# A graph layer on one core: the order of its head is rewritten

## The chip, the cores and the metric

The kernel runs on one NeuronCore of a Trainium2 chip. A core has TensorE (PE, matrix products; its weight loads are shown as PEld), VectorE (DVE), ScalarE (ACT), GpSimd (POOL) and SyncE (SP), which here only issues DMAs. All engines run their own instructions in order and wait for each other on semaphores; 16 DMA engines move data between device memory and the core's memory (SBUF). The metric is the device time of one execution in microseconds (us).

## The reference

A layer of a graph network over 3125 nodes with 256 channels and 103125 edges, in float32. The edges come sorted by their destination `dst`. What is computed, with names shortened:

```python
xn  = layernorm(x)                                   # per node
agg = segment_sum(xn[src], dst, 3125)                # sum over a node's incoming edges
h   = relu(agg @ W_rel + b_rel + xn @ W_root)        # 256 -> 512
i, f, g, o = split(h @ W_ih.T + b_ih + b_hh, 4)      # 512 -> 4 x 512, f is not used
hl  = sigmoid(o) * tanh(sigmoid(i) * tanh(g))
x   = x + (hl @ W_fc + b_fc) + mix(xn)               # mix: 8 heads, k and v normed, q @ (k^T v) / N + xn
# then a mixture of 8 experts, top 2 of a softmax per node, on layernorm(x):
x   = x + sum over the node's two experts of weight * (gelu(xe @ W1 + b1) @ W2 + b2)
```

## The kernel before, in words

The nodes are cut into 25 tiles of 126 (`T`, `P`). The aggregation is a matrix product: for a chunk of 252 destinations (13 chunks, the last shorter), a matrix `A` holds, for each pair of a source and a destination, how many edges join them, and the aggregated channels are the sum over the 25 source tiles of `xn^T A`. To keep float32's precision, `xn` is split into `hi` and `lo`, two operands of a reduced type, so each tile takes four products of 126x252 (L630: two halves of the channels, `hi` and `lo`).

`A` is built on the chip from lists of edges. Destinations are taken in groups of six, 525 groups in all, and each group may have up to 256 edges. `build` (L379 to L394) makes three groups' part of `A`: two comparisons on VectorE (L384, `hr` of sources and `hk` of keys), six products on PE (L390), one copy on ScalarE (L392). A chunk needs 14 builds. `hr` and `hk` have two buffers each, so VectorE can be at most two builds ahead of PE.

What stands ahead of the first chunk is called the head here. It does four things at once:

- **Loads.** SP loads `raw` (dst and src as a table of 128 rows with 808 edges each), the nodes `xn` in five loads of five tiles, `W_root`, `firsts` (row 0 of that table, the first edge of every column, copied to 105 partitions), `behind` and a dozen small vectors. They stand on SP's queue in the order of the program (L156 to L230).
- **Norms.** `norm(b)` (L343) normalizes five tiles: five pairs of L194 and L195 for the moments, a square root on ScalarE (L197), a reciprocal (L198), five writes (L349), and a store of the tiles to device memory. `rounded(b)` (L353) makes `hi` on ScalarE; L436 makes `lo` on VectorE.
- **Root products.** `root(t0)` (L358) takes four tiles: eight transposes on PE (L366), two copies on ScalarE (L368), then for each of four quarters `m` of the 512 channels a product in four passes on PE (L373) and a copy with the bias on ScalarE (L376), and stores of `xT` and of the four quarters to device memory (L369, L377). There are seven, the last with one tile. Products land in one of three PSUM buffers (`ps_mm`), shared with the builds; transposes in one of two (`ps_tr`), shared with those of the lists; the quarters wait in six buffers `hr` for their stores.
- **Lists.** `find()` (L236) is a generator that makes the lists of edges in steps, each ended by a `yield`. Step one: `raw` as float32 (L248), transposed on PE (L254) and stored as `ends_dram` in the order of the edges (L263, L265). Step two: five scans over `firsts` (L275) count on VectorE, for each group, the columns that begin below it; `at_i` is the column in which it starts, and five gathers on POOL (L283) fetch those columns as `near`. Step three: five scans over `near` (L289) give the exact first edge `begin_i` (L292), and five more gathers (L297) fetch each group's 256 edges as `both`. Step four, the rest: for each of the five sets of 105 groups, six operations on VectorE turn `both` into the tile of the source, the source within its tile and a key (L307 to L316); `order` and `wrong` (L321 to L324) check that the edges are sorted and no group is over-full; PE sums `wrong` over the partitions (L326), and `total_f`, `off` are made of it (L328, L330); then per set four transposes on PE (L336), and copies to `rowT` on ScalarE (L338) and `keyT` on VectorE (L340), which reads `off`.

The order of the work on an engine is made by a scheduler that takes the program's order as priority and issues what is ready by its own estimate. `tc.issue_after(ins)` puts all instructions of its block that run on the engine of `ins` behind it. In the head of the kernel before (L404 to L441) it is used three times: the first norm behind the store of `ends_dram`, step two behind the first norm's last write, the second norm behind `at_i`. `pins` hands such instructions out of `find`.

Behind the head, for every chunk, PE runs the 100 products of L630 with the 14 builds of the next chunk between them. VectorE and ScalarE also run the mixing part there, from a queue of steps keyed by chunk and build: `fetch` loads five tiles `q` from `xn_dram` (L510, from SP), `means` (L517) sums them on VectorE behind the twelfth build of the first chunk. At the end of each second chunk SP writes a blank part of `xs_dram` (7 MB). Weights for the network part behind the chunks, `wrel`, `wih` (three loads) and `wfc`, 4 MB together, are loaded from SP after the head's program (L445 to L452), into memory that the head's tiles have left.

Of the kernel before, what the change touches and what calls it, by code (L numbers as in the profile page):

```python
# [9 lines left out]
F32 = mybir.dt.float32  # L10
# [4 lines left out]
OP = mybir.AluOpType  # L15
AX = mybir.AxisListType

N = 3125
C = 256
P = 126  # L20
T = 25
# [42 lines left out]
def gps_layer(  # L64
# [90 lines left out]

    nc.sync.dma_start(raw[:, 0, :], dst)  # L156
    nc.sync.dma_start(raw[:, 1, :], src)
    for b in range(T // TB):
        load_nodes(xn[:, b * TB:(b + 1) * TB, :], b * TB, (b + 1) * TB)
        if b == 0:  # L160
            nc.sync.dma_start(wroot, W_root.rearrange("(k p) m -> p k m", p=128))
            nc.sync.dma_start(firsts, dst[0:1, :].to_broadcast([GP, NCP]))
            brel = columns_of(b_rel, KH, "brel")
# [73 lines left out]
    def find():  # L237
# [8 lines left out]
        for i in range(2):  # L246
            ends = sp.tile([128, NCP], F32, name="ends", tag="ends", bufs=2)
            nc.scalar.copy(ends, raw[:, i, :])  # L248
            for r in range(0, nr, 4):
                pt = ps_tr()  # L250
                m = min(4, nr - r)
                for j in range(m):
                    w = min(128, NCP - 128 * (r + j))
                    nc.tensor.transpose(pt[:w, 128 * j:128 * j + 128],  # L254
                                        ends[:, 128 * (r + j):128 * (r + j) + w], ident)
                whole_ = m if NCP >= 128 * (r + m) else m - 1
                if whole_:
                    nc.scalar.copy(rows[:, r:r + whole_, :, i],
                                   pt[:, :whole_ * 128].rearrange("p (r e) -> p r e", e=128))
                if whole_ < m:  # L260
                    nc.scalar.copy(rows[:left, r + whole_, :, i],
                                   pt[:left, whole_ * 128:m * 128])
# [10 lines left out]
        scr = sp.tile([GP, NCP], F32, name="scr", tag="ends", bufs=2)  # L273
# [18 lines left out]
        nc.vector.scalar_tensor_tensor(begin_i, at, 128.0, below, op0=OP.mult, op1=OP.add)  # L292
# [27 lines left out]
        order = sp.tile([128, NCP], F32, name="order", tag="ends", bufs=2)  # L320
# [3 lines left out]
        nc.vector.tensor_reduce(wrong[:, 1:2], full, AX.X, OP.add)  # L324
# [33 lines left out]
    def root(t0):  # L358
# [11 lines left out]
        for m in range(KH):  # L370
            pm = ps_mm()
            for k in range(KC):
                nc.tensor.matmul(pm[:, :n], wroot[:, k, 128 * m:128 * m + 128], xt[:, k, :n],  # L373
                                 start=(k == 0), stop=(k == KC - 1))
            hr = np_.tile([128, TQ * P], F32, name="hr", bufs=6)
            nc.scalar.activation(hr[:, :n], pm[:, :n], AF.Identity, bias=brel[:, m:m + 1])  # L376
            nc.sync.dma_start(root_dram[:, m, t0 * P:t0 * P + n], hr[:, :n])  # L377
# [25 lines left out]

    pins = []  # L404
    steps = find()
    next(steps)
    with tc.issue_after(pins.pop().ins):
        normed = norm(0)
    with tc.issue_after(normed.ins):
        next(steps)  # L410
    root(0)
    rounded(0)
    with tc.issue_after(pins.pop().ins):
        norm(1)
    next(steps)
# [3 lines left out]
    norm(2)  # L419
    root(2 * TQ)  # L420
    rounded(2)
    for _ in steps:
        pass
    norm(3)
    rounded(3)
    norm(4)
# [4 lines left out]
    root(3 * TQ)  # L431
    for _ in range(2):
        next(parts)
# [3 lines left out]
    for t0 in range(4 * TQ, T, TQ):  # L437
        root(t0)
        for _ in range(5):
            next(parts, None)  # L440
# [4 lines left out]
    nc.sync.dma_start(wrel, W_rel.rearrange("(k p) m -> p k m", p=128))  # L445
    wih = gl.tile([128, KH, 3, DH], F32, name="wih")

    wv = W_ihT.rearrange("(k p) m -> p k m", p=128)
    for i, gate in enumerate((0, 2, 3)):
        nc.sync.dma_start(wih[:, :, i, :], wv[:, :, gate * DH:(gate + 1) * DH])  # L450
    wfc = gl.tile([128, KH, C], F32, name="wfc")
    nc.sync.dma_start(wfc, W_fc.rearrange("(k p) m -> p k m", p=128))  # L452
# [663 lines left out]
```

## Time and profile before

| | us |
|---|---|
| median of 5 runs | 1148.34 (1147.43 to 1148.81) |
| the profiled execution's own time | 1152.27 |
| span of the profile, first to last instruction | 1150.5 |
| PE busy over the span | 1058.8 (92%) |
| DVE / ACT / POOL busy | 553.6 / 427.7 / 170.5 |
| mean granted TensorE clock | 0.966 |
| first product of the aggregation (L630) | 96.14 |
| start of chunks 2, 3 and 4 | 115.18, 133.78, 155.31 |

How to read the lines that follow: each names the start and the length in us, the engine (SPq and the like are an engine's DMA issues), the line of the kernel, the operation, `out<-in` with shapes, a count, and in brackets how long the engine had idled before and what ended that. In rows by stage, each engine's busy time is followed by its count of instructions in brackets; "PEclk" or the granted clock is the share of its full speed that TensorE was given. A copy is "lands" when its semaphore shows the last of its parts.

### The profile page before, as it was taken

The page shows a single profiled execution, that of the slowest core. Times are in us where ns is not written, and L with a number is a line of the kernel's source. Part 1 is how long each engine was busy: PE and PEld are TensorE (multiplying, and loading weights), DVE is VectorE, ACT ScalarE, POOL GpSimd, SP SyncE. Part 2 cuts the span into 40 slices and gives each one's busy share as a digit, 9 for nine tenths or more (in the row PEclk, how much of TensorE's full clock was granted, in tenths as well). Part 3 has the DMA queues.
Part 4 walks back from the last instruction along what each step waited for, and adds up shares of the span by engine and source line. Part 5 has one row for each costly group of instructions (what it writes and reads, how often), then busy time and mean ns, then how long its engine had stood idle before and what let it go on. Part 6 is the DMA issues. An engine that isn't in the chain of part 4 may idle for free. (4 is left out here: it accounts for less than half of the span.)

```text
span 1150.5 us, 15551 instructions
## 1 busy us (share of the span) xinstructions
PE 1058.8 (92%) x5613; PEld 809.1 (70%) x5613; DVE 553.6 (48%) x1767; ACT 427.7 (37%) x936; POOL 170.5 (15%) x153
## 2 busy tenths in 40 slices
PE   5799999999999999999999997399999999999992
PEld 3358998998995454555555457288888888788781
DVE  5757788787751183939393927411112222221210
ACT  3454754764722233333333336122222222223120
POOL 2220000000001002020202022112222212221221
PEclk9799999999999999999999999599999999999996
DMA  7983964872008321212121111157666667766734
GB/s 230 302 290 107 252 199 115 234 209 57 1 1 282 131 91 37 90 38 91 37 91 38 35 38 58 40 169 202 192 191 189 183 205 207 215 188 161 225 66 124
DMA packets 121148, 161.43 MB, mean 140 GB/s; under 512 B 9570, under 2 KB 109320, under 8 KB 120870
## 3 DMA queue, kind: packets, MB, share of 16 engines
q1 hardware_dynamic: 108156, 144.40, 39.9%
q0 software_dynamic: 12064, 15.08, 7.0%
q8 instruction: 49, 0.80, 0.3%
q10 hardware_dynamic: 840, 0.83, 0.2%
q14 instruction: 39, 0.32, 0.1%
HBM read 101.37 MB, written 62.10 MB: 142 GB/s over the span
## 5 line engine op out<-in xcount | busy, mean ns | idle before, releaser
L747 PE MATMUL ps_mm<-hT,wih 128*128 128x504 f32 (+1 forms) x672 | 259.3, 546 | 0.1
L747 PEld LDWEIGHTS ps_mm<-hT,wih 128*128 128x128 f32 x672 | 121.8, 193 | 132.3 <-issue 127.9
L1020 PE MATMUL ps_mm<-xe,w 128*128 128x256 f32 (+1 forms) x896 | 190.5, 371 | 3.5 <-DVE xe L1014 3.5
L1033 PE MATMUL ps_o<-w,hf 128*128 128x256 f32 x832 | 184.2, 379 | 0.0
L1020 PEld LDWEIGHTS ps_mm<-xe,w 128*128 128x128 f32 x896 | 162.5, 193 | 27.5 <-DVE xe L1014 6.8
L630 PE MATMUL ps_o<-A,hi 126*128 126x252 f32 (+1 forms) x650 | 175.8, 304 | 0.8 <-ACT A L392 0.7
L1033 PEld LDWEIGHTS ps_o<-w,hf 128*128 128x128 f32 x832 | 157.8, 190 | 21.3
L630 PE MATMUL ps_o<-A,lo 126*128 126x252 f32 (+1 forms) x650 | 160.9, 280 | 0.0
L1022 ACT ACTIVATE hf<-ps_mm,sm 128x256 f32<-128x256 f32 (+1 forms) x160 | 71.7, 453 | 201.7 <-PE ps_mm L1020 200.0
L392 ACT CAST A<-ps_mm 126x450 fp32r<-126x450 f32 x175 | 93.8, 538 | 99.7 <-PE ps_mm L390 98.1
L1038 POOL DMA_INDIRECT acc_dram<-y,xs x52 | 80.4, 1546 | 322.4 <-DVE y L1037 114.4
L630 PEld LDWEIGHTS ps_o<-A,hi 126*128 126x128 f32 x650 | 124.4, 191 | 2.8 <-ACT aggT L638 1.7
L384 DVE TENSOR_TENSOR hr<-two,rowT 128x756 bf16<-128x756 bf16 x175 | 95.8, 548 | 62.0 <-PE ps_mm L390 61.5
L630 PEld LDWEIGHTS ps_o<-A,lo 126*128 126x128 f32 x650 | 124.9, 192 | 0.0
L390 PE MATMUL ps_mm<-hk,hr 128*126 128x150 bf16 x1050 | 102.5, 233 | 12.7 <-DVE hk L384 12.4
L384 DVE TENSOR_TENSOR hk<-two,keyT 128x900 bf16<-128x900 bf16 x175 | 108.7, 621 | 0.0
L390 PEld LDWEIGHTS <-hr 128*126 128x126 bf16 x1050 | 91.9, 138 | 18.5 <-DVE hk L384 16.5
L1036 DVE TENSOR_TENSOR y<-ps_o,b2s 128x256 f32<-128x256 f32 x52 | 22.1, 425 | 158.7 <-PE ps_o L1033 158.7
L749 ACT ACTIVATE act<-ps_mm,bg 128x504 f32<-128x504 f32 (+1 forms) x84 | 52.6, 634 | 107.3 <-PE ps_mm L747 96.4
L795 DVE SCALAR_TENSOR_TENSOR scr<-xl,wrows 126x256 f32<-126x256 f32 x160 | 75.5, 472 | 3.3
L872 POOL DMA_INDIRECT xs_dram<-rows,at_i x50 | 52.7, 1053 | 128.3 <-DVE at_i L869 110.5
L1022 ACT ACTIVATE hf<-ps_mm,small 128x256 f32<-128x256 f32 x64 | 29.9, 474 | 77.1 <-PE ps_mm L1020 77.1
(250 smaller groups left out, 919.4 us busy)
## 6 DMA issues: line engine op xcount, KB each, us to landing
w<-in_W_dram SPq DMA_DIRECT2D x56, 1024.0 KB
xs_dram<-blank SPq DMA_DIRECT2D x3, 7022.5 KB
xs_dram<-blank SPq DMA_DIRECT2D x1, 6757.5 KB
xs<-xs_dram SPq DMA_DIRECT2D x24, 265.0 KB
root_dram<-hr SPq DMA_DIRECT2D x24, 252.0 KB
root<-root_dram SPq DMA_DIRECT2D x6, 1008.0 KB
b2s<-in_b_dram SPq DMA_DIRECT2D x28, 128.0 KB
xn_dram<-xn SPq DMA_DIRECT2D x5, 630.0 KB
```

The costliest lines, as they stand in the source:

```text
L384: row = nc.vector.tensor_tensor(to[:, :m], two[:, :, :w, :].to_broadcast([128, m, w, GH]), of[:, g:g + m, None, :].to_broadcast([128, m, w ...
L390: mm = nc.tensor.matmul(pa[:P, i * DT:(i + 1) * DT], hr[:, i, :, h], hk[:, i, :, h], start=(h == 0), stop=(h == GH - 1))
L392: copy = nc.scalar.copy(A[:, :, c0:c0 + m * D], pa[:P, :m * DT].rearrange("p (d t) -> p t d", t=T))
L630: last = nc.tensor.matmul(pg[k][:, :n], of[:, t, 128 * k:128 * k + 128], A[:, t, :n], start=(t == 0 and of is hi), stop=(t == T - 1 and of ...
L747: mm = nc.tensor.matmul(pm[:, :n], wih[:, k, i, 128 * m:128 * m + 128], hT[:, k, :n], start=(k == 0), stop=(k == KH - 1))
L749: nc.scalar.activation(act[:, i, :n], pm[:, :n], AF.Tanh if gate == 2 else AF.Sigmoid, bias=bg[:, gate, m:m + 1])
L795: nc.vector.scalar_tensor_tensor(scr, xl[:, i, :], 1.0, wrows[:, e, :], op0=OP.mult, op1=OP.mult, accum_out=lg[:, i, e:e + 1])
L872: put = nc.gpsimd.indirect_dma_start(out=xs_dram[:, :], out_offset=bass.IndirectOffsetOnAxis(ap=at_i[:w, i:i + 1], axis=0), in_=rows[:w, i ...
L1020: nc.tensor.matmul(pm, w1[:, k, 128 * m:128 * m + 128], xe[:, k, :], start=(k == 0), stop=(k == KC - 1))
L1022: nc.scalar.activation(hf[:, m, :], pm, AF.Gelu, bias=b1s[:, m:m + 1])
L1033: nc.tensor.matmul(po, hf[:, m, 128 * h:128 * h + 128], w2[:, m, :], start=(m == 0), stop=(m == KF - 1))
L1038: nc.gpsimd.indirect_dma_start(out=acc_dram[:, :], out_offset=bass.IndirectOffsetOnAxis(ap=xs[:, h, C + NE:].bitcast(I32), axis=0), in_=y, ...
```

## The change

Six edits, all in the head.

1. `firsts` is loaded first on SP, ahead of `raw`; before, it stood behind the first load of nodes and `W_root`.
2. `ends`, `scr` and `order` share three buffers instead of two, so that the scans of `firsts` need not wait for the transposes of `ends`.
3. The chain of orders is longer (`then(ins, do, ...)` runs a step behind an instruction). The scans and the gathers of `near` come straight behind the store of `ends_dram` in the program, without a wait for a norm; norm 0 is put behind `at_i`, norm 1 behind the last write of norm 0, the step of `begin_i` and the gathers of `both` behind the last write of norm 1, norm 2 behind `begin_i`, norm 3 behind norm 2, the work on `both` behind norm 3, norm 4 behind the last operation on `wrong`.
4. `find` has one more `yield`, behind `wrong`; what follows it (the sum on PE, the transposes of the lists, `rowT`, `keyT`) is put, on PE, behind the second quarter of the fourth root product (`root(3 * TQ, lambda: ...)`), so it stands in the middle of that product.
5. The builds of the first chunk: before, 2 behind the fourth root product and 5 behind each later one; now 3 inside and 3 behind the fifth, 5 inside and 3 behind the sixth, none around the last.
6. The loads of `wrel`, `wih` and `wfc` are put on SP behind the last store of the last root product.

In the order that results, VectorE runs the five scans of `firsts` ahead of the first norm; a `lo` (L444) stands inside norm 1, one between the last scan of `near` and `begin_i`, one inside norm 3, one ahead of `total_f`; on SP the store of `xn` from norm 3 stands ahead of the third root product's stores, and the five weight loads stand ahead of the first two loads of `q`; on POOL the gathers of `both` stand ahead of the additions for `bg` and the copies to `small`. Behind the head every engine's order is the same as before. Lines move by up to 10: L373 is L375, L349 is L351, L436 is L444, L384 is L390, L517 is L526, L630 is L639.

```diff
@@ -153,13 +153,13 @@
         nc.sync.dma_start(of, ap)
         return of
 
+    nc.sync.dma_start(firsts, dst[0:1, :].to_broadcast([GP, NCP]))
     nc.sync.dma_start(raw[:, 0, :], dst)
     nc.sync.dma_start(raw[:, 1, :], src)
     for b in range(T // TB):
         load_nodes(xn[:, b * TB:(b + 1) * TB, :], b * TB, (b + 1) * TB)
         if b == 0:
             nc.sync.dma_start(wroot, W_root.rearrange("(k p) m -> p k m", p=128))
-            nc.sync.dma_start(firsts, dst[0:1, :].to_broadcast([GP, NCP]))
             brel = columns_of(b_rel, KH, "brel")
 
     nc.sync.dma_start(behind[:112, :], dst[1:113, :])
@@ -244,7 +244,7 @@
         nc.gpsimd.memset(rows[:, nf, :, 0], float(FAR))
         nc.gpsimd.memset(rows[:, nf, :, 1], 0.0)
         for i in range(2):
-            ends = sp.tile([128, NCP], F32, name="ends", tag="ends", bufs=2)
+            ends = sp.tile([128, NCP], F32, name="ends", tag="ends", bufs=3)
             nc.scalar.copy(ends, raw[:, i, :])
             for r in range(0, nr, 4):
                 pt = ps_tr()
@@ -270,7 +270,7 @@
 
 
         below = sp.tile([GP, GQ], F32, name="below")
-        scr = sp.tile([GP, NCP], F32, name="scr", tag="ends", bufs=2)
+        scr = sp.tile([GP, NCP], F32, name="scr", tag="ends", bufs=3)
         for q in range(GQ):
             nc.vector.tensor_scalar(scr, firsts, limit[:, q:q + 1], None, op0=OP.is_lt, op1=OP.add,
                                     accum_out=below[:, q:q + 1])
@@ -289,7 +289,8 @@
             nc.vector.tensor_scalar(scr[:, :128], near[:, q, :, 0], limit[:, q:q + 1], None,
                                     op0=OP.is_lt, op1=OP.add, accum_out=below[:, q:q + 1])
         begin_i = sp.tile([GP, GQ], I32, name="begin_i")
-        nc.vector.scalar_tensor_tensor(begin_i, at, 128.0, below, op0=OP.mult, op1=OP.add)
+        pins.append(nc.vector.scalar_tensor_tensor(begin_i, at, 128.0, below,
+                                                   op0=OP.mult, op1=OP.add))
 
 
         both = sp.tile([GP, GQ, GE, 2], F32, name="both", tag="both")
@@ -317,11 +318,12 @@
                                            op0=OP.mult, op1=OP.add)
 
         wrong = const.tile([128, 2], F32, name="wrong")
-        order = sp.tile([128, NCP], F32, name="order", tag="ends", bufs=2)
+        order = sp.tile([128, NCP], F32, name="order", tag="ends", bufs=3)
         nc.vector.tensor_tensor(order, raw[:, 0, :], behind, OP.is_gt)
         nc.vector.tensor_reduce(wrong[:, 0:1], order, AX.X, OP.add)
 
-        nc.vector.tensor_reduce(wrong[:, 1:2], full, AX.X, OP.add)
+        pins.append(nc.vector.tensor_reduce(wrong[:, 1:2], full, AX.X, OP.add))
+        yield
         pw = ps_tr()
         nc.tensor.matmul(pw[:, :2], ones, wrong, start=True, stop=True)
         total_f = const.tile([128, 1], F32, name="total_f")
@@ -355,7 +357,7 @@
         s = slice(TB * b, TB * b + TB)
         nc.scalar.copy(hi[:, s, :], xn[:, s, :])
 
-    def root(t0):
+    def root(t0, between=None):
 
         ts = range(t0, min(T, t0 + TQ))
         n = len(ts) * P
@@ -370,11 +372,15 @@
         for m in range(KH):
             pm = ps_mm()
             for k in range(KC):
-                nc.tensor.matmul(pm[:, :n], wroot[:, k, 128 * m:128 * m + 128], xt[:, k, :n],
-                                 start=(k == 0), stop=(k == KC - 1))
+                mm = nc.tensor.matmul(pm[:, :n], wroot[:, k, 128 * m:128 * m + 128], xt[:, k, :n],
+                                      start=(k == 0), stop=(k == KC - 1))
             hr = np_.tile([128, TQ * P], F32, name="hr", bufs=6)
             nc.scalar.activation(hr[:, :n], pm[:, :n], AF.Identity, bias=brel[:, m:m + 1])
-            nc.sync.dma_start(root_dram[:, m, t0 * P:t0 * P + n], hr[:, :n])
+            store = nc.sync.dma_start(root_dram[:, m, t0 * P:t0 * P + n], hr[:, :n])
+            if between and m == KH // 2 - 1:
+                with tc.issue_after(mm.ins):
+                    between()
+        return store
 
     def build(A, g, c0, m):
 
@@ -401,55 +407,58 @@
         for d in range(d0, d1, BANK * D):
             yield build(A, d // D, d - d0, min(BANK, (d1 - d) // D))
 
+    def then(ins, do, *of):
+
+        with tc.issue_after(ins.ins):
+            return do(*of)
+
+
     pins = []
     steps = find()
     next(steps)
+    stored = pins.pop()
+    next(steps)
     with tc.issue_after(pins.pop().ins):
-        normed = norm(0)
-    with tc.issue_after(normed.ins):
-        next(steps)
+        last = then(stored, norm, 0)
     root(0)
     rounded(0)
-    with tc.issue_after(pins.pop().ins):
-        norm(1)
-    next(steps)
+    last = then(last, norm, 1)
+    then(last, next, steps)
     nc.vector.tensor_copy(two[:, 0], two_f[:, :, None].to_broadcast([128, DT, GH]))
     root(TQ)
     rounded(1)
-    norm(2)
+    last = then(pins.pop(), norm, 2)
+    last = then(last, norm, 3)
     root(2 * TQ)
     rounded(2)
-    for _ in steps:
-        pass
-    norm(3)
     rounded(3)
-    norm(4)
+    then(last, next, steps)
+    root(3 * TQ, lambda: next(steps, None))
+    then(pins.pop(), norm, 4)
     rounded(4)
     found.close()
 
     parts = builds(A0, 0)
-    root(3 * TQ)
-    for _ in range(2):
-        next(parts)
     for b in range(T // TB):
         u = slice(b * TB, b * TB + TB)
         nc.vector.tensor_tensor(lo[:, u, :], xn[:, u, :], hi[:, u, :], OP.subtract)
-    for t0 in range(4 * TQ, T, TQ):
-        root(t0)
-        for _ in range(5):
+    for t0, n in zip(range(4 * TQ, T, TQ), (3, 5, 0)):
+        stored = root(t0, lambda: [next(parts) for _ in range(n)])
+        for _ in range(3):
             next(parts, None)
     nodes.close()
 
     gl = ctx.enter_context(tc.tile_pool(name="gl", bufs=1, side="right"))
     wrel = gl.tile([128, KC, DH], F32, name="wrel")
-    nc.sync.dma_start(wrel, W_rel.rearrange("(k p) m -> p k m", p=128))
     wih = gl.tile([128, KH, 3, DH], F32, name="wih")
+    wfc = gl.tile([128, KH, C], F32, name="wfc")
 
     wv = W_ihT.rearrange("(k p) m -> p k m", p=128)
-    for i, gate in enumerate((0, 2, 3)):
-        nc.sync.dma_start(wih[:, :, i, :], wv[:, :, gate * DH:(gate + 1) * DH])
-    wfc = gl.tile([128, KH, C], F32, name="wfc")
-    nc.sync.dma_start(wfc, W_fc.rearrange("(k p) m -> p k m", p=128))
+    with tc.issue_after(stored.ins):
+        nc.sync.dma_start(wrel, W_rel.rearrange("(k p) m -> p k m", p=128))
+        for i, gate in enumerate((0, 2, 3)):
+            nc.sync.dma_start(wih[:, :, i, :], wv[:, :, gate * DH:(gate + 1) * DH])
+        nc.sync.dma_start(wfc, W_fc.rearrange("(k p) m -> p k m", p=128))
 
 
     wrT = gl.tile([NE, C], F32, name="wrT")
```

## The prediction

> **What bounds the kernel now.** I read the page's slices first, then the order of time over the first 115 us, then busy time by stage, and last the landings in the trace's semaphore events.
>
> ```profile
> PE   5799999999999999999999997399999999999992
> PEclk9799999999999999999999999599999999999996
> ```
>
> A slice is 28.8 us. TensorE is nearly full behind the third slice; the first three are the head. By stage, PE is busy 9.02 + 16.74 + 14.37 + 19.50 + 13.73 = 73.4 of the first 96 us, so at most 22.6 us are there to gain. The order of time shows what PE waits for:
>
> ```profile
> 10.06 0.75 DVE L194 BATCH_NORM_STATS2 bn<-xn 126x6 f32<-126x256 f32 x2 [7.81 <-DMA xn<-in_x_dram]
> ...
> 14.58 1.05 DVE L275 TENSOR_SCALAR_CACHE_REDUCE scr<-firsts,limit 105x808 f32<-105x808 int32 x1
> ...
> 22.05 1.20 POOL L283 DMA_INDIRECT near<-ends_dram,at_i  x1 [19.83 <-DVE bn L194]
> ...
> 33.57 0.18 DVE L292 SCALAR_TENSOR_TENSOR begin_i<-at,below 105x5 int32<-105x5 f32 x1
> ...
> 50.28 0.15 DVE L324 TENSOR_REDUCE wrong<-full 128x1 f32<-128x5 f32 x1
> ...
> 58.89 0.43 DVE L340 TENSOR_SCALAR keyT<-ps_tr,off 128x210 bf16<-128x210 f32 x1
> ...
> 60.27 8.02 PE L373 MATMUL ps_mm<-xt,wroot 128*128 128x504 f32 x16
> ...
> 96.14 0.39 PE L630 MATMUL ps_o<-A,hi 126*128 126x252 f32 x1 [0.65 <-ACT A L392]
> ```
>
> VectorE idles until 10.06, then does the scans of `firsts`, then the list chain (first gather 22.05, `begin_i` 33.57, `wrong` 50.28, last `keyT` 58.89), with norms between. The third product ends at 48.65 and the fourth starts only at 60.27, behind the lists. The first aggregation is at 96.14. Busy time by stage adds the clock (columns: PE, PEld, DVE, ACT, POOL busy, granted clock, DMA share, GB/s):
>
> ```profile
> 24.93:28.34 3.41, 1.82 (x7) 0.61 (x5) 1.61 (x9) 0.09 (x1) 2.80 (x3) 1.00 0.40 107
> 28.34:31.75 3.41, 1.74 (x6) 1.34 (x7) 2.51 (x13) 2.79 (x4) 0.14 (x1) 0.50 0.66 161
> 48.82:52.23 3.41, 0.90 (x6) 0.76 (x6) 3.41 (x15) 0.62 (x2) 0.00 (x0) 1.00 0.99 339
> 52.23:55.65 3.42, 0.99 (x5) 0.67 (x5) 3.42 (x13) 2.28 (x4) 0.00 (x0) 0.50 0.79 287
> ```
>
> A stretch of 3.41 us with PE about half busy is followed by one at half clock, where a pass of L373 takes 0.84 us for 0.42.
>
> What comes after the head is needed too, since the change moves loads there:
>
> ```profile
> 97.02 0.89 SPq L510 DMA_DIRECT2D q<-xn_dram  x2
> ...
> 110.00 1.48 DVE L517 TENSOR_REDUCE hmean<-q 126x40 f32<-126x1280 f32 x1
> ...
> 112.74 0.63 PE L390 MATMUL ps_mm<-hk,hr 128*126 128x150 bf16 x6 [0.59 <-DVE hk L384]
> ```
>
> `hmean` runs 13.9 us behind the first aggregation, and PE already waits 0.59 us for the build behind it: VectorE has no slack there.
>
> **The change part by part.** The new program's order on each engine is known; I put the durations above into it. Root products are counted 0 to 6.
>
> *`firsts` first.* `raw` of dst landed at 4.08, that of src, equally large, at 5.38: 404 KB in 1.30 us. The 331 KB ahead of them cost 1.07 us: dst 5.15, src 6.45, the first `xn` 11.1 for 10.06. `firsts` itself lands near 3.9, and its five scans (1.09 apart), `two` 0.2 and `at`, `at_i` 0.4 end at 10.0 instead of 21.7, in time when VectorE was idle. Root 0 starts at 17.5 (16.49), ends at 26.3 (25.83).
>
> *Norms in one piece.* Norm 1 could follow norm 0 at 15.6, but its load landed at 19.26; it starts there (21.63 before). Stats 2.0, one `lo` 1.4 that the new order puts inside, square root and reciprocal 0.65, five writes 1.6: done at 24.9 (28.9). PE goes from root 0 to root 1: transposes to 27.4, ScalarE's copies behind one `hi` and three `hr` to 28.5, product 28.5 to 35.3 (31.32 to 39.66).
>
> *The gathers.* `ends_dram` landed at 18.77, now about 19.8; `near` starts there instead of 22.05. The slowest DMA channel of SP's queue was behind until 26.53, and the first gather landed on it at 26.70. I take 26.7 to 27.5 for all five. Bounds: 2.6 us behind each issue (other channels in this trace), or the last at 32.2 as before. Scans end at 28.7, a `lo` of 1.4 stands ahead of `begin_i`: 30.3 (33.57). `both` follows on POOL at 30.6 (34.57), now ahead of `bg` and `small`, for which nothing on the path waits.
>
> *Norms 2 and 3.* Both now stand behind `begin_i`. Norm 2 from 30.3, first write 2.9 later as in norm 0 (10.06 to 12.96), last at 34.9. ScalarE's `hi` follows to 36.1, then a `lo` inside norm 3 to 37.9; norm 3's square root is at 38.1, and on ScalarE the last `hr` of root 1 and the copies for root 2 are queued behind it. So root 2 starts at 39.4 (41.53), after 3 us of idle PE. By the rows above that costs the clock: at half rate to about 45.4, end 49.2 (48.65). Kept, it would end at 46.2.
>
> *Lists behind norm 3, transposes inside root 3.* Norm 3 ends at 40.3. `both` landed 4.9, 7.2, 10.6, 12.8 and 13.8 us behind its first issue; from 30.6 the last is in at 44.4, and five groups of 1.4 to 1.6 us, `order` 1.8 and `wrong` end at 49.5 (50.28) without waiting for it. Root 3 starts at 51.2; its first eight passes end at 54.6, and only there the sum of `wrong` is taken on PE. `total_f` comes at 55.0 (53.11), the last `keyT` 5.8 us later as before: 60.8 (58.89). The other eight passes, 3.4 us, run between the list transposes. Root 3 ends at 60.8, not 67.7. This is where the gain lies: the lists end later than before, but a root product is behind PE by then.
>
> *The rest of the head.* From root 4's first transposes (68.97) to 96.14 were 27.2 us. Added are two builds that stood ahead (0.84) and 0.6 where groups of 3, 3, 5, 3 builds wait for VectorE oftener than 2, 5, 5, 2; the wait of 0.65 at the end goes, as root 6 now stands behind the last build. 60.9 + 27.2 + 0.84 + 0.6 − 0.65 = 88.9. Gain of the head: 96.14 − 88.9 = 7.2 us.
>
> *The weights behind the last store.* `wrel`, `wih` and `wfc`, 4096 KB, leave the head, where SP's stores no longer queue behind them; by these times no `hr` buffer waits longer. But on SP they now stand ahead of `q`. Before, the last store of `root_dram` was issued at 95.17 and `q` landed at 101.42: 6.25 us, of which 1.85 the wait for the store. Loads moved 300 (`wih` behind `wrel`) to 350 KB/us: 12 to 14 us more. The last store is now 0.6 us behind the first aggregation, so `q` is in at 0.6 + 6.25 − 1.85 + 12 to 14 = 17.0 to 19.0, and `hmean` was due at 13.9. Builds for the second chunk stand behind it on VectorE, PE behind those: 3.1 to 5.1 us lost, 4.1 taken. Bounds: nothing, if `q` is not held up; 9.7, in the second rival.
>
> The skill's page "DMA: Bandwidth & Descriptors", section "Queues, rings and completion order", says that a DMA engine takes a queue's descriptors in ring order, which speaks against this edit. The trace has it for loads only (the two `q` at 101.42 and 103.39, in order); by the rule 4.1 us are lost, with no such order up to nothing, and the sum would be 1141.1.
>
> **Sum.** 7.2 − 4.1 = 3.1 us faster. Profiled: span 1150.5, time 1152.27, 3.9 above the median of the runs; the difference goes to the median: 1148.34 − 3.1 = 1145.2.
>
> The skill's page "TensorE: Matmul & The Clock Gate", Part 1, says that the clock drops after an idle window of about 3.4 us. The trace drops it after a half busy one (1.82 of 3.41, above). By the rule root 2 would stay at full clock and end at 46.2, root 3's half would be at 51.7, `total_f` be set by VectorE at 53.0, and the sum be 2.0 us lower, 1143.2.
>
> **The rivals.**
> *The gathers land early* (2.6 us behind each issue) and the clock holds in root 2. For it: channels other than the slowest did so. Against: the slowest decides. `begin_i` 29.3, root 2 a microsecond earlier, and 2.0 for the clock: 3.0 more, 1142.2.
> *The weights hold the builds longer* (other side). If they move at the 263 GB/s of the stage from 70 to 80 us, they take 16.0 us and `q` lands at 21; `hmean` is 7.1 late, and PE, idle that long, pays one and a half windows of half clock, 2.6. 9.7 − 7.2 = 2.5 slower: 1150.8. It decides from a loss of 7.2 on. Against: that stage was shared with stores.
> *The head gains, the hold-up takes it back*: loss at 5.1 and one window of half clock (1.7): 0.4 faster, 1147.9. For it: the half busy rows.
> *The last `near` lands as late as before* (32.2): everything from norm 2 on 3.6 later; gain 3.6, loss 4.1: 1148.8.
>
> **How the numbers follow.** Forecast 0.45, early gathers 0.15, longer hold-up 0.12, taken back 0.18, late `near` 0.10. Range 1139.5 to 1150.5: below the early case by the 2.7 that a `q` not held up in full would add, above up to the slower case. The forecast's own range is 1143 to 1147. 0.2% of 1148 is 2.3 us, about what a measurement of this kernel can tell. Beyond 2.3 faster: most of the forecast and the early case, 0.57; within: 0.27; slower: 0.16.
>
> **What would show it.** `at_i` near 10; the first gather near 20; `begin_i` near 30; PE idle ahead of root 2, with a half clock stage; `keyT` ending near 61 between passes of L375; the first aggregation at 87 to 91; `hmean` waiting for DMA `q`, PE for VectorE about 17 us into the aggregation. Wrong if the first aggregation is later than 92, or if `hmean` starts on time.

## The result and the profile after

The changed kernel takes 1151.58 us (median of 28 runs, 1148.44 to 1154.51), the kernel before 1148.06 us in the runs beside it (53, 1144.91 to 1152.19). The ratio is 1.0028, 95% interval 1.0021 to 1.0035: slower by 0.28%, 3.2 us, where 1145.2 and 3.1 us faster were forecast. The profiled execution has a span of 1151.4 us and a time of 1153.22.

The slices of the page show no stage that has changed its kind; each is 28.8 us, too coarse for what happened.

```profile
PE   5897999999999999999999999299999999999991
...
PEclk9899999999999999999999999599999999999996
```

The order of time of the changed kernel shows the same steps as before (start, duration, engine, line, operation; in brackets the idle time ahead and what ended it):

```profile
11.16 0.17 DVE L280 CAST at_i<-at 105x5 int32<-105x5 f32 x1
...
22.70 1.21 POOL L283 DMA_INDIRECT near<-ends_dram,at_i  x1 [20.48 <-DVE xn L351]
...
33.99 0.16 DVE L292 SCALAR_TENSOR_TENSOR begin_i<-at,below 105x5 int32<-105x5 f32 x1
...
53.42 3.65 PE L375 MATMUL ps_mm<-xt,wroot 128*128 128x504 f32 x8 [0.43 <-ACT xt L370]
53.59 0.42 DVE L317 SCALAR_TENSOR_TENSOR both<-both,st__445 105x256 f32<-105x256 f32 x1
53.93 0.15 DVE L325 TENSOR_REDUCE wrong<-full 128x1 f32<-128x5 f32 x1
...
62.56 0.43 DVE L342 TENSOR_SCALAR keyT<-ps_tr,off 128x210 bf16<-128x210 f32 x1 [0.20 <-ACT rowT L340]
...
91.24 0.36 PE L639 MATMUL ps_o<-A,hi 126*128 126x252 f32 x1
```

`at_i` is 10 us earlier, yet `begin_i`, `wrong` and the last `keyT` are 0.4, 3.7 and 3.7 us later than before. The fourth root product now starts at 53.42 for 60.27, and its first eight passes lie behind PE before the lists are done. The first aggregation starts at 91.24 for 96.14: in this pair of executions the head gains 4.9 us. Then the first chunk, from the first aggregation to the start of the second chunk's, takes 27.5 us for 19.0. SP's queue, the waits from 91 to 130 us (waiter, releaser: total, times, longest) and three rows in order of time, the last of them the start of the second chunk, say why:

```profile
90.62 1.75 SPq L379 DMA_DIRECT2D root_dram<-hr  x4
92.42 0.42 SPq L458 DMA_DIRECT2D wrel<-in_W_rel_dram  x1
92.89 2.05 SPq L460 DMA_DIRECT2D wih<-in_W_ihT_dram  x3
94.99 1.17 SPq L461 DMA_DIRECT2D wfc<-in_W_fc_dram  x1
96.34 7.53 SPq L519 DMA_DIRECT2D q<-xn_dram  x2
```

```profile
DVE hmean L526 <- DMA q<-xn_dram: 5.9, 1, 5.9
...
PE ps_mm L396 <- DVE hk L390: 7.0, 2, 6.6
```

```profile
111.70 1.49 DVE L526 TENSOR_REDUCE hmean<-q 126x40 f32<-126x1280 f32 x1 [5.91 <-DMA q<-xn_dram]
...
114.46 1.01 PE L396 MATMUL ps_mm<-hk,hr 128*126 128x150 bf16 x6 [6.59 <-DVE hk L390]
...
118.71 0.28 PE L639 MATMUL ps_o<-A,hi 126*128 126x252 f32 x1
```

The semaphore events give the landings: `wrel` 97.31, `wih` 100.03, 104.27 and 107.44, `wfc` 109.59, the first `q` 111.68. `hmean` starts at 111.70, 20.5 us behind the first aggregation; before it was 13.9. The builds for the second chunk stand behind it on VectorE, and PE stands behind those. Busy time by stretch shows what stands still behind it (PE, PEld, DVE, ACT, POOL busy, granted clock, DMA share, GB/s):

```profile
104.50:108.00 3.50, 3.37 (x34) 3.17 (x32) 1.29 (x3) 1.62 (x3) 0.00 (x0) 1.00 1.00 289
108.00:111.70 3.70, 0.00 (x0) 0.00 (x0) 0.00 (x0) 0.00 (x0) 0.00 (x0) 1.00 0.70 196
111.70:115.15 3.45, 0.69 (x6) 0.69 (x7) 3.41 (x6) 0.00 (x0) 0.00 (x0) 0.52 0.03 9
115.15:118.71 3.56, 3.56 (x21) 3.56 (x20) 2.44 (x5) 1.23 (x3) 0.00 (x0) 0.51 0.02 5
```

For 3.7 us none of the five engines is busy; the next 7 us run at half clock. This is the course that the second rival, the longer hold-up, described, though not for the reason that it gave (below).

### The profile page after: what moved, and what is told of

Same layout as the page of the kernel before. It is cut to its first block, busy times and chain, and to the rows that moved or that the text cites. A ratio compares the mean times of both kernels' runs of the same rounds, so it can differ in the third digit from the quotient of the medians.

```text
span 1151.4 us, 15558 instructions
## 1 busy us (share of the span) xinstructions
PE 1057.6 (92%) x5613; PEld 809.9 (70%) x5613; DVE 555.3 (48%) x1767; ACT 426.9 (37%) x936; POOL 164.8 (14%) x153
## 5 line engine op out<-in xcount | busy, mean ns | idle before, releaser
L639 PE MATMUL ps_o<-A,hi 126*128 126x252 f32 (+1 forms) x650 | 178.0, 307 | 0.0
L639 PE MATMUL ps_o<-A,lo 126*128 126x252 f32 (+1 forms) x650 | 162.6, 282 | 0.0
L639 PEld LDWEIGHTS ps_o<-A,hi 126*128 126x128 f32 x650 | 126.4, 194 | 1.6 <-ACT aggT L647 1.5
L639 PEld LDWEIGHTS ps_o<-A,lo 126*128 126x128 f32 x650 | 126.6, 195 | 0.0
L390 DVE TENSOR_TENSOR hr<-two,rowT 128x756 bf16<-128x756 bf16 x175 | 95.8, 548 | 56.7 <-PE ps_mm L396 55.8
L396 PE MATMUL ps_mm<-hk,hr 128*126 128x150 bf16 x1050 | 103.9, 235 | 20.0 <-DVE hk L390 19.4
L390 DVE TENSOR_TENSOR hk<-two,keyT 128x900 bf16<-128x900 bf16 x175 | 108.8, 621 | 0.0
L375 PE MATMUL ps_mm<-xt,wroot 128*128 128x504 f32 (+1 forms) x112 | 51.2, 605 | 7.7 <-ACT xt L370 4.3
```

Source lines behind the costliest of these rows:

```text
L390: row = nc.vector.tensor_tensor(to[:, :m], two[:, :, :w, :].to_broadcast([128, m, w, GH]), of[:, g:g + m, None, :].to_broadcast([128, m, w ...
L396: mm = nc.tensor.matmul(pa[:P, i * DT:(i + 1) * DT], hr[:, i, :, h], hk[:, i, :, h], start=(h == 0), stop=(h == GH - 1))
L639: last = nc.tensor.matmul(pg[k][:, :n], of[:, t, 128 * k:128 * k + 128], A[:, t, :n], start=(t == 0 and of is hi), stop=(t == T - 1 and of ...
```

## The experiments

Theory W: the 4096 KB of weights ahead of `q` on SP hold up `hmean` and are the whole loss. Rival H: the new head leaves the aggregation a worse start. In the first four kernels the order on PE, VectorE, ScalarE and POOL is that of their base; only SP's differs. All ratios are against the kernel before, timed beside each kernel: its median was 1148.38 us beside these four, 1148.12 beside the next four and 1146.89 beside the last three. Between these groups the ratios compare better than the times. Line numbers in the rows are those of each run's own kernel.

**The changed kernel, its weights back in the head.**

```diff
-    with tc.issue_after(stored.ins):
-        nc.sync.dma_start(wrel, ...)
+    nc.sync.dma_start(wrel, ...)
...
```

> The changed kernel with the loads of wrel, wih and wfc back in the head, as the kernel before issues them; the instructions of all other engines keep their order. Theory W (the 4096 KB ahead of q on SP hold up hmean, and that is the whole loss): hmean starts 13 to 14.5 us behind the first aggregation instead of 20.5, the first chunk takes 19 to 19.5 us instead of 27.5, no half clock stage at 112 to 119; the first aggregation moves from 91.2 to at most 93, because stores queue behind the weights again; the time is 3 to 5 us below the kernel before, 1143 to 1145. Rival H (the new order of the head leaves the aggregation a worse start, through builds or clock, and the weights only happen to lie there): the first chunk stays at 26 to 28 us and the time at 1150 to 1153.

Measured: 1143.53 us, ratio 0.9960 (0.9947 to 0.9973). First aggregation 89.24, `hmean` 14.0 behind it, first chunk 19.2. Theory W; rival H is out.

**The kernel before, with its weights behind the last store alone.**

```diff
-    nc.sync.dma_start(wrel, ...)
+    with tc.issue_after(stored.ins):
+        nc.sync.dma_start(wrel, ...)
...
```

> The kernel before with one part of the change: wrel, wih and wfc issued behind the last store of the last root product. Theory W: hmean starts 20 to 21 us behind the first aggregation instead of 13.9, the first chunk takes 26.5 to 28 us instead of 19.0, and the time is 7 to 10 us above the kernel before, 1155 to 1158, less up to 1.5 if the head's stores gain by it. Rival H: the first chunk stays near 19 to 21 us, the time within 2 us of the kernel before.

Measured: 1156.98 us, 1.0082 (1.0063 to 1.0100). First aggregation 95.61, `hmean` 18.5 us behind it, first chunk 25.5, both a little less than theory W said (20 to 21, 26.5 to 28): the trace has 6.5 us of loss in the first chunk, the time 8.6. The loss arises in the old head as well. Its waits from 95 to 130 us:

```profile
PE ps_mm L391 <- DVE hk L385: 5.3, 1, 5.3
```

**The changed kernel, its weights behind `q`.**

```diff
-    with tc.issue_after(stored.ins):
+    def weights(b):
+        with tc.issue_after(batches[b][-1].ins):
...
-                (0, 7, fetch), (0, 11, means), ...
+                (0, 7, fetch), *([(0, 7, weights)] if b == 1 else []), (0, 11, means), ...
```

> The changed kernel with the weights issued behind the two q loads instead of ahead of them; nothing else moves. Theory W: the first aggregation stays at 91 to 91.5, hmean is due 13 to 14.5 us behind it, the first chunk takes 19 to 19.5 us, the second 21.5 to 22; the time is 4 to 6 us below the kernel before, 1142 to 1144, the whole gain of the head. Rival H: first chunk 26 to 28 us, time 1150 to 1153. Rival D (the weights delay whatever moves beside them, wherever they stand in the order): q lands 3 to 10 us later than 6.3 us behind its issue, and the time is 1146 to 1150.

Measured: 1143.00 us, 0.9953 (0.9940 to 0.9966). SP's queue and the wait of PE from 91 to 130 us:

```profile
91.03 1.75 SPq L379 DMA_DIRECT2D root_dram<-hr  x4
94.33 0.89 SPq L521 DMA_DIRECT2D q<-xn_dram  x2
95.25 0.48 SPq L459 DMA_DIRECT2D wrel<-in_W_rel_dram  x1
95.78 3.33 SPq L461 DMA_DIRECT2D wih<-in_W_ihT_dram  x3
99.15 4.36 SPq L462 DMA_DIRECT2D wfc<-in_W_fc_dram  x1
```

```profile
PE ps_mm L396 <- DVE hk L390: 0.8, 2, 0.6
```

`q` lands at 98.88, 7.2 us behind the first aggregation (91.65) for 20.4, and PE's wait is 0.8 for 7.0; `hmean` starts 14.3 us behind the first aggregation, the first chunk takes 19.4. Here `batches[b][-1]` is the second load of `q`. The same loads, behind it in the queue instead of ahead, gain 1151.58 − 1143.00 = 8.6 us; in the old head, being ahead costs 1156.98 − 1148.38 = 8.6 us too. Rival D is out: the weights still move beside the aggregation, and `q` lands 4.6 us behind its issue.

**The kernel before, its weights behind `q`.** The same edit on the kernel before.

> The kernel before with the weights issued behind the two q loads, the head's order as before. It prices what the weights cost inside the old head. Theory W: the first chunk stays at 19 to 19.5 us; the first aggregation comes at 95 to 96.2 for 96.1; the time is 0 to 1.5 us below the kernel before. Rival S (stores queued behind the weights held the old head's root products through their buffers): the first aggregation comes at 92 to 94.5, the time 2 to 4 us below.

Measured: 1148.47 us, 1.0002 (0.9993 to 1.0012). First aggregation 97.16, first chunk 19.0. Rival S is out: inside the old head the weights cost nothing that shows in the time; there was nothing to free by moving them.

So the change is two separate things: a head worth 1143.00 − 1148.38 = −5.4 us and weights worth +8.6. The next kernels ask which part of the head gives the gain. Their base is the changed kernel with its weights behind `q`. One caution on their traces: four kernels with the same head (the changed one and three with other places for the weights) began their first aggregation at 91.24, 89.24, 91.65 and 88.11 us, three with the old head at 96.14, 95.61 and 97.16. A shift of this point under some 3 us tells little in one execution; the means are 90.1 and 96.3, 6.2 apart.

**List transposes ahead of the fourth product.**

```diff
-    root(3 * TQ, lambda: next(steps, None))
+    next(steps, None)
+    root(3 * TQ)
```

> The changed kernel with its weights behind the q loads (1143.0 us, first aggregation 91.65), and in it one part undone: the sum of wrong and all list transposes ahead of the fourth root product instead of inside it. Theory L (the head's gain lies in the fourth product, whose first eight passes run while VectorE still works on the lists): the fourth product starts at 59 to 61 instead of 52, the first aggregation comes at 95 to 98, the time is 1146.5 to 1149.5, so most of the 5.4 us are gone. Rival G (the gain comes from the earlier norms and the builds' places, the lists hide anyway): first aggregation 91.5 to 93.5, time 1142.5 to 1145.

Measured: 1147.61 us (1142.26 to 1151.00), 0.9995 (0.9979 to 1.0010): the gain is gone, as theory L has it. But the profiled execution is the one of 1142.26, with the first aggregation at 92.31, as rival G has it. I repeated the edit on another base (small loads later, below):

> The changed kernel with weights behind q and the small loads behind the first root product (1141.6 us, first aggregation 87.6), and the list transposes ahead of the fourth root product. The same edit on the base with early small loads left open what it is worth: its runs had a median 4.6 us higher, its one profiled execution a first aggregation only 0.7 us later, in an execution that began 1.7 us earlier. Theory L: the fourth product starts at 56 to 58 instead of 49.4, the first aggregation comes at 91 to 93.5, the time is 1145 to 1147.5. Rival G (the fourth product is shorter when nothing interrupts it, 6.8 to 8 us instead of 11, and that gives nearly all back): first aggregation 88.5 to 90, time 1142 to 1144.

Measured: 1147.64 us, 1.0005 (0.9988 to 1.0022), against 1141.63 for that base. This time the trace shows it too: first aggregation 96.20 for 87.60. The fourth product in both kernels, the first list first:

```profile
55.24 0.72 PE L338 MATMUL ps_tr<-ident,both 105*128 105x105 f32 x4 [0.41 <-DVE keyT L342]
...
57.56 7.01 PE L375 MATMUL ps_mm<-xt,wroot 128*128 128x504 f32 x16
```

```profile
52.53 0.35 PE L310 MATMUL ps_tr<-wrong,ones 128*128 128x2 f32 x2 [2.99 <-DVE wrong L307]
...
59.64 8.84 PE L357 MATMUL ps_mm<-xt,wroot 128*128 128x504 f32 x16
```

And busy time by stretch of the second (columns as above):

```profile
49.80:53.20 3.40, 0.67 (x6) 0.70 (x7) 3.20 (x10) 0.51 (x1) 0.00 (x0) 1.00 1.04 384
53.20:56.60 3.40, 3.01 (x16) 2.31 (x16) 2.59 (x10) 1.34 (x4) 0.00 (x0) 0.51 0.48 166
56.60:60.10 3.50, 2.83 (x13) 2.28 (x12) 3.04 (x8) 1.13 (x3) 2.64 (x6) 0.50 0.00 0
60.10:63.50 3.40, 3.40 (x5) 1.32 (x4) 2.80 (x9) 0.81 (x3) 0.70 (x7) 0.50 0.42 154
```

With the transposes ahead, PE waits 3 us for `wrong`, and here the clock was then halved for three stretches, up to 63.5. In the execution of 1142.26 the third product ran at half clock and longer (9.99 us), ended only as `wrong` came, and the clock stayed full from 47.9 on. That this alternative makes the spread of the runs is likely, but two traces do not show it. Theory L holds by time in both pairs, 4.6 and 6.0 us (4.8 and 6.1 by the ratios); in the second trace the first aggregation is later than it said (91 to 93.5).

**The parts on `firsts` undone.** `firsts` behind `wroot`, as before, and:

```diff
     next(steps)
     stored = pins.pop()
-    next(steps)
-    with tc.issue_after(pins.pop().ins):
-        last = then(stored, norm, 0)
+    last = then(stored, norm, 0)
+    then(last, next, steps)
     root(0)
     rounded(0)
-    last = then(last, norm, 1)
+    last = then(pins.pop(), norm, 1)
```

> The same base (weights behind q, 1143.0 us), and in it the parts on firsts undone: firsts loaded behind wroot, its five scans behind the norm of the first tiles, the second norm behind at_i, as the kernel before has it. Theory N (the chain of the head runs through the last near gather, which landed at 32.2 in the kernel before and in the changed one, so the early firsts buy almost nothing): at_i at 21 to 22, the second root product at 31 to 32 instead of 28.7, begin_i still at 33.5 to 34.5, the third product at 42 to 44.5, the first aggregation within 1 us of 91.65, the time 1142 to 1144.5. Rival F (early firsts and norms in one piece carry a good part of the head's gain): first aggregation 93.5 to 96, time 1145 to 1148.

Measured: 1142.67 us, 0.9956 (0.9937 to 0.9975), `at_i` 21.32, second product 28.23, `begin_i` 33.26, first aggregation 90.12 (the last three earlier than theory N said). Theory N by time: the early firsts and their scans buy nothing measurable. The traces show that the order moved by more than the edit names: the last four list transposes stand two passes of the fourth product earlier, and `total_f` ahead of the fifth norm's sums. What these did is not shown apart. On the other base, with small loads later:

> The same base (weights behind q, small loads later, 1141.6 us), with the parts on firsts undone: firsts loaded behind wroot, its scans behind the first norm, the second norm behind at_i. With the small loads in the way these parts bought nothing (1142.7 against 1143.0). Theory N2 (they buy something once the last near gather follows its issue: the first gather then waits for at_i at 21.3 instead of for ends_dram, 20.2): first near at 21.5 to 22, begin_i 1 to 1.5 us later than 31.7, the first aggregation at 88.3 to 89.5, time 1142 to 1143.5. Rival Z (they buy nothing here either, since the load ahead of dst costs what the earlier scans bring): first aggregation 86.5 to 88, time 1140.5 to 1142.

Measured: 1139.81 us, 0.9943 (0.9930 to 0.9957), first aggregation 88.09 against 87.60, `begin_i` 33.45 against 31.68. By time it is below both, next to rival Z; by `begin_i` it is theory N2. A `begin_i` that came 1.8 us later cost no time here, but the list transposes and `total_f` have moved as in the kernel above, so this is not shown for `begin_i` alone.

**Small loads behind the first product.** The block from `wcol` to `ofs` stands under `with tc.issue_after(first_store.ins):` behind the second norm, `first_store` being what `root(0)` returns.

> The same base (weights behind q), with the dozen small loads (wcol, wrow, bfc, bg, bg2, wr, brb, of) issued behind the first root product's last store instead of at 20 to 32 us, beside the near gathers. Theory S (these loads, running from 25.5 on, hold up the last near gather, which lands 5.2 us behind its issue for 3 us of the fourth): the last near lands at 29 to 30.5 instead of 32.0 to 32.8, begin_i at 31 to 32.3 instead of 34.2, the first aggregation at 89 to 90.5, the time 1140.5 to 1142. Rival T (any transfer there does it, and the stores of norm and product that move up take the small loads' place): the last near at 31.5 to 33, first aggregation 91 to 92.5, time within 1 us of 1143.

Measured: 1141.63 us, 0.9952 (0.9937 to 0.9966) for 0.9953 of the base: no difference by time. The first aggregation is at 87.60, and the last gather is in at 30.0:

```profile
25.51 0.97 POOL L265 DMA_INDIRECT near<-ends_dram,at_i  x1 [0.30 <-issue]
...
30.00 0.35 DVE L271 TENSOR_SCALAR_CACHE_REDUCE scr<-near,limit 105x128 f32<-105x128 f32 x1 [1.24 <-DMA near<-ends_dram,at_i]
```

But one kernel with the early small loads (2560 KB ahead of `q`, below) had it at 30.4 and its first aggregation at 88.11. (In the base the last gather landed 4.4 us behind its issue, 28.04 to 32.45, not 5.2 as the text above has it.) Theory S is not shown, and rival T is not either; inconclusive.

**`firsts` third.**

```diff
-    nc.sync.dma_start(firsts, dst[0:1, :].to_broadcast([GP, NCP]))
     nc.sync.dma_start(raw[:, 0, :], dst)
     nc.sync.dma_start(raw[:, 1, :], src)
+    nc.sync.dma_start(firsts, dst[0:1, :].to_broadcast([GP, NCP]))
```

> The same base (weights behind q), with firsts loaded third, behind the two loads of raw instead of ahead of them. It tests the step that failed: the prediction let ends_dram land at 19.8 and the first near gather start there; it came at 22.7. Theory E (ends_dram is late because dst and src land 1.1 later, and the first gather waits for ends_dram): ends_dram is issued at 9.1 to 10.3 instead of 11.4, at_i comes at 12 to 12.6, the first near gather starts at 20 to 21.5. If the last gather follows its issue as before, begin_i comes at 32 to 33, the first aggregation at 90 to 91, the time 1141.5 to 1143. Rival K (the last gather lands at 32 whatever its issue): begin_i 33.5 to 34.5, time 1142.5 to 1144.5.

Measured: 1146.40 us, 0.9987 (0.9973 to 1.0002), slower than its base by 3.4; PE, VectorE, ScalarE and POOL keep their order. The first gather starts at 20.01 and `begin_i` comes earlier than theory E said, which ends rival K; but the time that E saw in it did not come:

```profile
30.61 0.16 DVE L292 SCALAR_TENSOR_TENSOR begin_i<-at,below 105x5 int32<-105x5 f32 x1
...
42.74 0.68 ACT L378 ACTIVATE hr<-ps_mm,brel 128x504 f32<-128x504 f32 x1 [5.64 <-DMA root_dram<-hr]
...
45.78 8.79 PE L375 MATMUL ps_mm<-xt,wroot 128*128 128x504 f32 x16 [6.81 <-ACT xt L370]
```

`begin_i` is at 30.61, 3.4 us earlier than in the changed kernel and where the prediction put it, but the third product starts at 45.78, not at 39.4. The earlier `both` gathers go out ahead of the stores: the first `root_dram` store behind them took 8.07 us to land, and ScalarE waited 5.64 us for a free `hr`, with PE behind it; between 28 and 52 us such waits are 6.6 us here and 1.2 in the base. Behind the wait the third product ran in part at half clock (42.5 to 49.4) and took 8.79 us for 7.03. `firsts` third also puts `at_i` at 13.88, and with it the first norm and product 2 us back. How the 3.4 us divide among these is not shown. In the changed kernel the DMA engines are as full there (share 0.98 to 1.03, here 0.97 to 1.02):

```profile
34.00:38.00 4.00, 0.95 (x2) 0.50 (x2) 3.60 (x17) 0.87 (x2) 2.42 (x3) 0.84 0.98 338
38.00:42.00 4.00, 3.44 (x12) 1.69 (x10) 3.98 (x13) 2.41 (x3) 3.37 (x5) 0.73 1.00 332
42.00:46.00 4.00, 2.60 (x4) 1.09 (x5) 3.62 (x15) 3.08 (x5) 0.48 (x3) 0.70 1.03 326
```

**A part of the weights ahead of `q`.** `wrel` and two thirds of `wih`, 2560 KB, behind the last store; the rest behind `q`.

> The changed kernel with 2560 of the 4096 KB (wrel and two thirds of wih) ahead of the q loads and the rest behind them: a dose between 0 and 4096 KB. Without weights ahead, q landed 7.2 us behind the first aggregation and hmean started at 14.3 (first chunk 19.4); with all of them q landed at 20.4, hmean started at 20.5 (27.5). Theory W (a plain queue: q lands later by the time that the KB ahead of it take, 13.2 us for 4096 KB, so 8.2 for 2560, and only what passes 14.3 costs anything): q lands at 15 to 16, hmean starts at 15.2 to 16.2, the first chunk takes 20 to 22 us, the time is 0.5 to 2.5 us above 1143.0. Rival P (the loss is in proportion to the KB): hmean at 18 to 19, first chunk 24 to 25, 4.5 to 5.5 us above.

Measured: 1144.94 us, 0.9986 (0.9973 to 0.9998): 1.9 us above the base by the medians, 3.8 by the ratios, since the kernel before took 1146.89 beside it. The first is inside theory W's range, the second between the theories; the trace has to decide. Its waits from 88 to 118 us:

```profile
PE ps_mm L396 <- DVE hk L390: 2.7, 2, 2.1
```

`q` landed 16.1 us behind the first aggregation, `hmean` started at 16.2, the first chunk took 22.4, 3.0 more than the base, of which 1.9 are the later `hmean`; the rest falls to one stretch of half clock (108.2 to 111.6). That is at theory W's upper bounds or a little over them; rival P, proportion, is out by its 18 to 19 and 24 to 25. It fits a queue with a threshold: by estimate some 7 us (14.3 − 7.2), or about 2200 KB at the 13.2 us that 4096 KB took, would have been free. No run has that dose.

The best kernel of the series is the one with weights behind `q`, small loads later and the parts on `firsts` undone: 1139.81 us, 0.9943 of the kernel before, and 0.85% under the changed one (0.9943 / 1.0028). Its interval overlaps that of the changed kernel with its weights alone behind `q`; that one edit is what is shown.

## Why the prediction was wrong

The direction was wrong because of one term, the weights: 4.1 us taken, 8.6 measured. Of the 6.3 us between 3.1 faster and 3.2 slower, 4.5 are this term; the other 1.8 are the head, 7.2 forecast and 5.4 by time, which alone would have left the kernel faster.

- *The term in detail.* `q` was put at 0.6 + 6.25 − 1.85 + 12 to 14 = 17.0 to 19.0 behind the first aggregation; it came at 20.4. The price of the KB was right: 20.4 against 7.2 without weights, 13.2 us. The last store was issued 0.7 behind the first aggregation, also right. The failed step is the 1.85 taken off for the wait on that store: from the last store's issue to `q`'s landing the kernel with weights behind `q` took 6.5 us, wait included, and the changed kernel 19.7, 13.2 more, so nothing of the 1.85 came back in the total. `wrel`, issued at 92.42 without the wait, landed only at 97.31, 4.9 us for 512 KB, and the 3584 KB behind it took 12.3. Why that first load is so slow is not shown.
- *What a late `hmean` costs.* This is the second failed step: it was counted at its lateness, the half clock behind it at nothing. It came 6.2 us later than in the kernel with weights behind `q` (20.5 for 14.3), and the first chunk was 8.0 longer. The two stretches of half clock fit the other 1.8: the 3.56 us of work in the second would be 1.8 at full clock. The half busy rows of the profile before were quoted for exactly this and used in the rivals, but not in the sum. The 0.6 us from 8.0 to the 8.6 by time are not placed.
- *The second rival* had the course (a `q` at 21, half clock behind the wait) and nearly the price, 9.7, and ended at 1150.8; it got 0.12. Its reason did not hold: it let the weights move at 263 GB/s and take 16.0 us, and they took 13.2, the forecast's own price. That it came so near is in part luck: its rate was too low by more than the 1.85 that it, too, took off.
- *The other rivals.* The last `near` did land as late as before, at 32.20, but the head gained 4.9 to 5.4 us, not the 3.6 that this rival gave it. The gain taken back had a loss of 5.1 and one window of half clock; it was 6.2 and two.
- *The signs.* Neither sign of a wrong prediction appeared: the first aggregation came ahead of 92 and `hmean` did not start on time. They watched for a lost gain and for no hold-up, not for a longer one.
- *Ring order.* The rule of the Trainium skill that was weighed ("DMA: Bandwidth & Descriptors", "Queues, rings and completion order") holds for these loads: `q` landed behind all weights ahead of it, at 111.68 behind `wfc`'s 109.59, and with 2560 KB ahead at 104.25, between the second `wih` (101.15) and the third (109.90).
- *The clock rule.* "TensorE: Matmul & The Clock Gate", Part 1, asks for an idle window; the stretch 108.0 to 111.7, PE 0.00, is one, and the half clock follows it, so here rule and trace agree. The stretch with 0.67 of 3.40 busy shows that a whole one is not needed. By the rule root 2 would have kept the full clock; it ran at half from 43.56 to 46.98, behind a window with PE busy 1.45 of 3.41 us. The prediction's own reading, that a half busy stretch costs the clock, does not always hold either (last section).
- *The head.* 7.2 was forecast, 4.9 came in the profiled pair, 6.2 as a mean of like heads, and 5.4 by time. `firsts` first: `at_i` 11.16 for 10.0, since `firsts` landed at 5.22 for 3.9, and worth nothing that was measured. Norm 1 started at 16.08 for 19.3 and was done at 21.85 for 24.9. The 19.26 was a misreading: in the kernel before, that load's last part came at 16.13, and 19.26 is the first count of the next copy on the same semaphore. It gained nothing, since root 1 waited for PE and not for the norm (28.77 for 28.5). The gathers failed: the first went out at 22.70 for 19.8. `raw` of dst landed at 6.23 for 5.15, so `ends_dram` was issued 2.3 us later than before and landed at 21.7, and `begin_i` came at 33.99 for 30.3. Root 3 started at 53.42 for 51.2; from root 4's transposes (62.86 for 60.9) to the first aggregation it took 28.4 us for the 28.0 summed. So 2.0 of the missing 2.3 us lie ahead of root 4.
- *An earlier `begin_i`.* The kernel that put it at 30.6 suggests that the next step would have failed too: the DMA engines are full behind it, which the prediction didn't count, and an earlier `begin_i` moves the gathers ahead of the stores.
- *The wait on ScalarE* came one norm earlier than said: ScalarE stood 7.0 us for the sums of norm 2, root 1's `hr` copies were queued behind the square root, and PE idled 3.0 us ahead of 37.16. Root 2 started at 43.40, not 39.4, and ran in part at half clock, as said.
- *Root 3 with the lists inside* was named as the place of the gain, and is: taking it out costs 4.6 and 6.0 us. That the lists end later than before (62.56 for 58.89) was right as well.
- *The store relief* was put at nothing, and the old head with its weights behind `q` gives nothing (1.0002).

## What to carry to other kernels

A load that is moved off one queue's busy stage lands in front of whatever that queue issues next: look up what the next load is, when its reader is due, and how many KB the slack between the two holds, from the issue of the last transfer ahead and not from the bare rate. Where PE will stand still for some 3.4 us, add the half clock behind it to the sum, not to a rival. And when one edit mixes an order of work with a move of loads, test the two apart: here two places in a queue turned 0.28% slower into 0.47% faster.

## What the runs showed of the hardware

- The granted clock changes in steps of 3.41 us. Cut into windows at these steps, from 10 to 250 us in the thirteen traces: at full clock, every window with PE busy less than 1.40 us was followed by half clock, and none with more than 1.92 us. Between the two both occur: 1.82 (kernel before, 24.9 to 28.3) was, 1.57 and 1.61 (2560 KB ahead of `q`, 36.5 to 43.4) were not. So the busy share of one window does not decide by itself, and what else does is open.
- The half clock can last beyond its cause. In the second kernel with the list transposes ahead it held for three stretches, 53.2 to 63.5, though PE was busy 3.01 of 3.40 and 2.83 of 3.50 us in the first two; the full clock came back behind the one with 3.40 of 3.40. But in the changed kernel a window at half clock with 2.99 of 3.41 (36.7 to 40.2) was enough.
- 4096 KB of loads beside the aggregation need not delay it when nobody waits for them: with the old head the first chunk took 19.0 us with most of them moving beside it (the last landed 1.5 us behind its end), and 19.0 without.
- The same head, in four kernels that differ only in loads, began the aggregation within a spread of 3.5 us (88.11 to 91.65). One profiled execution cannot price an edit of a microsecond there.
